# Paired attention products, shared tiles, and a last target block in two narrow passes: a change to a four-layer graph network

## The chip, the cores and the metric

The kernel runs on one core of one Trainium2 chip. The core's engines are called PE (TensorE, matmuls; PEld is its weight load), DVE (VectorE), ACT (ScalarE), POOL (GpSimd) and SP (which issues loads). SBUF is the on-chip memory, PSUM the accumulator memory that TensorE writes.

## The reference

Four layers work on 4096 nodes with 128 features and one 4096 x 4096 weighted adjacency matrix, stored in full in float32. After each layer comes a residual addition and a layer norm. The change touches the third layer (attention with 4 heads of 32 features), the end of the second, and how the fourth is run beside the third:

```
# layer 2 (the third): attention
C    = alpha_src[None, :, :] + alpha_dst[:, None, :]
tau  = adj.T[..., None] * exp(maximum(0.2 * C, C))
att  = tau / sum(tau, axis=1)
z    = einsum('mnh,nhf->mhf', adj.T[..., None] * att, h_prime) + bias
# layer 3 (the fourth)
out  = h @ W_self + (adj @ h / clip(sum(adj, 1), 1)) @ W_neigh
```

## The kernel before

A *step* takes 128 source nodes (`nt`, 32 of them), 2 heads and 1024 target nodes. ACT copies the tile `a` of the adjacency to PSUM. DVE makes two scores `tau`, maximum and multiplication in one instruction each, and part of `tau2 = tau * a`; POOL makes the rest. TensorE then adds up `den` from `tau` and `num` from `tau2`, with matmuls of 32 output columns. Thirty-two steps are a *pass*; eight passes cover 4 groups of 1024 targets and 2 pairs of heads.

```
def load(self, nt):
    if nt % 2 == 0:
        self.a2 = ld.tile([P, 2, WB], F32, name="chunk")
        nc.sync.dma_start(self.a2, adj[self.mp, nt // 2])
    a = self.a2[:, nt % 2, :]
    ap = ps_a[nt % len(ps_a)].tile([P, WB], F32, name="a")
    nc.scalar.activation(ap, a, AF.Copy, accum_out=deg[:, nt, self.mp:self.mp + 1])
    return a, ap

def products():
    if len(behind) > 1:
        heads, nt, tau, _ = behind[-2]          # den: one step behind
        heads.product(True, nt, tau)
    if len(behind) > 2:
        heads, nt, _, tau2 = behind.popleft()   # num: two steps behind
        heads.product(False, nt, tau2)
        # ... cut: end of a pass

# cut: step() = scores, the next load, then products()
while todo:
    step()
    credit = min(credit + 1.3, 2.0) if pieces else 0.0
    while credit >= 1.0:                        # matmuls of layer 3
        credit -= 1.0
        if one(pieces):
            credit = 0.0
    one(chains)                                 # small work: D, transposes, norms
```

The order on each engine is the order of this program. While the second layer's product with `w` runs on TensorE (8 blocks of 32 full matmuls), the first 46 steps are placed between its matmuls; from pass 2 on, the product of the fourth layer fills TensorE in *pieces* of one full matmul each. `tau` and `tau2` have three buffers each.

The softmax here doesn't subtract the row's maximum and nothing guards it: scores larger than these inputs give would overflow.

Of the kernel before, what the change touches and what calls it, by code (L numbers as in the profile page):

```python
# [33 lines left out]
def adj_resnorm_d4(ctx: ExitStack, tc: tile.TileContext, x_in, xT_in, adj, adjT, w0g, w0gT, a0, w1a, b1a,  # L34
# [56 lines left out]
    deg = const.tile([P, NT, NW], F32, name="deg")  # L91
# [383 lines left out]
    def network(usual):  # L475

        with ExitStack() as whole:
# [98 lines left out]

            ps_nd = enter(name="ps_nd", bufs=1, space=PSUM)
# [10 lines left out]
            def block_end(ib, p):  # L588
# [3 lines left out]
                oT = l1w.tile([P, IB], F32, name="t2T")  # L592
                nc.vector.tensor_add(oT, p, h0T[:, blk])
                elu(oT, oT, B1B)
# [34 lines left out]
            def block_targets(ib):  # L629

                blk = slice(ib * IB, (ib + 1) * IB)
                pd = ps_x.tile([96, IB], F32, name="px")
                nc.tensor.matmul(pd, WD, xT[:, blk], start=True, stop=True)
                d = l1w.tile([96, IB], F32, name="elu_r")
                nc.scalar.activation(d, pd, AF.Exp, scale=-0.8)
                nc.scalar.copy(dv[:, blk], d)
                yield
                yield
                nc.vector.tensor_sub(d, d, dv[:, blk])
                nc.scalar.copy(dv[32:64, blk], d[32:64, :])  # L640
                nc.scalar.copy(dv[64:96, blk], d[64:96, :])
                yield
                nc.vector.tensor_sub(d[64:96, :], d[64:96, :], dv[64:96, blk])
                nc.scalar.copy(dv[64:96, blk], d[64:96, :])
                yield
# [4 lines left out]
            class Heads:  # L650
# [3 lines left out]
                def __init__(self, mp, hp):  # L654
                    self.mp, self.hp = mp, hp
                    self.D, self.made = None, 0
                    self.sums = ps_first if (mp, hp) == (0, 0) else ps_nd

                def load(self, nt):

                    if nt % 2 == 0:
                        self.a2 = ld.tile([P, 2, WB], F32, name="chunk")
                        nc.sync.dma_start(self.a2, adj[self.mp, nt // 2])
                    a = self.a2[:, nt % 2, :]
                    ap = ps_a[nt % len(ps_a)].tile([P, WB], F32, name="a")
                    nc.scalar.activation(ap, a, AF.Copy, accum_out=deg[:, nt, self.mp:self.mp + 1])  # L666
                    return a, ap

                def targets(self, mbs=range(2)):
                    if self.D is None:  # L670
                        self.D = l2w.tile([P, 2, 2, IB], F32, name="D", bufs=2)
                    for mb in mbs:
                        for h in range(2):
                            d = ps_x.tile([P, IB], F32, name="px")
                            nc.tensor.matmul(d, selD[:, 2 * self.hp + h, :],
                                             dv[:, self.mp * WB + mb * IB:self.mp * WB + (mb + 1) * IB],
                                             start=True, stop=True)
                            nc.scalar.copy(self.D[:, h, mb, :], d)
                            self.made += 1
                            yield  # L680

                def step(self, nt, a, ap):

                    assert self.made == 4
                    tau = l2w.tile([P, 2, WB], F32, name="tau", bufs=3)
                    tau2 = l2w.tile([P, 2, WB], F32, name="tau2", bufs=3)
                    for h in range(2):
                        nc.vector.scalar_tensor_tensor(tau[:, h, :], self.D[:, h].rearrange("p b i -> p (b i)"),  # L688
                                                       es[:, nt, 2 * self.hp + h:2 * self.hp + h + 1], ap,
                                                       op0=ALU.max, op1=ALU.mult)  # L690
                    nc.vector.tensor_tensor(tau2[:, 0, 0:OWN], tau[:, 0, 0:OWN], ap[:, 0:OWN], ALU.mult)  # L691
                    nc.gpsimd.tensor_tensor(tau2[:, 0, OWN:WB], tau[:, 0, OWN:WB], a[:, OWN:WB], ALU.mult)  # L692
                    nc.gpsimd.tensor_tensor(tau2[:, 1, :], tau[:, 1, :], a, ALU.mult)  # L693
                    return tau, tau2

                def product(self, is_den, nt, r):
# [5 lines left out]
                    for h in range(2):  # L702
                        for mb in range(2):
                            q = 32 * (2 * h + mb)
                            nc.tensor.matmul(acc[q:q + 32, :], weights(nt, 2 * self.hp + h, is_den),  # L705
                                             r[:, h, mb * IB:(mb + 1) * IB], start=nt == 0, stop=nt == NT - 1)
                    if nt == NT - 1:
                        if is_den:
                            self.nd = l2w.tile([P, 2, IB], F32, name="nd")
                        nc.scalar.copy(self.nd[:, int(is_den), :], acc)  # L710

                def finish(self):
# [8 lines left out]
                    z = l2w.tile([P, TB, 2, 2, FO], F32, name="z")  # L721
                    nc.vector.tensor_mul(z.rearrange("p k h b f -> p (k h b) f"),
                                         q.rearrange("p k (g f) -> p (k g) f", f=FO),
                                         rd.rearrange("p k g -> p (k g)")[:, :, None].to_broadcast([P, TB * 4, FO]))
                    for mb in range(2):
                        xb = x[:, (2 * self.mp + mb) * TB:(2 * self.mp + mb + 1) * TB,
# [216 lines left out]
```

## Time and profile before

The median of before is 2280.9 us (2279.25 to 2281.45, beside the changed kernel). The end of the trace, cut by marks: t0 is DVE's addition at the end of the first block of the product with `w`; the other marks are the starts of DVE's own product (`tau2`) in steps 64, 192 and 256.

| stretch | us | what sets it |
|---|---|---|
| t0 to step 64 | 414.0 | TensorE beside the product with `w`, then DVE and ACT by turns |
| step 64 to 192 (passes 2 to 5) | 420.1 | DVE, without idle time |
| step 192 to 256 (passes 6, 7) | 213.1 | DVE, without idle time |
| step 256 to the end (tail) | 94.3 | TensorE finishing layer 3 |

### The profile page before, as it was taken

What the parts mean: (1) busy time and instruction counts of PE and PEld (TensorE: products, weight loads), DVE (VectorE), ACT (ScalarE), POOL (GpSimd) and SP (SyncE); (2) the same over time, 40 slices, a digit from 0 to 9 for tenths busy, and PEclk for the clock granted to TensorE, in tenths of its full rate; (3) what the DMA queues carried; (4) which work ended last, traced back from release to release, by engine and by line L of the source; (5) the groups of instructions that cost most, each with busy time, mean ns of one, the idle gap of its engine ahead of it and who ended that gap; (6) DMA issues with size and microseconds to landing.
All of it is one profiled execution on the core that took longest, in us unless ns stands there. A gap on an engine that the chain in (4) does not pass through costs nothing.

```text
span 2278.0 us, 22715 instructions
## 1 busy us (share of the span) xinstructions
PE 2176.3 (96%) x8552; PEld 843.0 (37%) x8552; DVE 1176.9 (52%) x1709; ACT 593.6 (26%) x1012; POOL 836.9 (37%) x540
## 2 busy tenths in 40 slices
PE   4899999999999999999999999879999999999998
PEld 3333444444444444444443333212222322232233
DVE  4554462000010110000026777779999999999955
ACT  4764200000000000000032222334444443443320
POOL 0000000000000000000004555669999999999930
PEclk9899999999999999999999999999999999999999
DMA  7886658889777677778876556434666666666665
GB/s 279 336 334 232 213 178 273 300 299 302 266 256 242 233 263 242 263 266 271 274 245 230 201 186 220 167 111 149 223 254 241 224 244 243 243 234 238 238 226 203
DMA packets 83608, 549.14 MB, mean 241 GB/s; under 512 B 9376, under 2 KB 15520, under 8 KB 17568
## 3 DMA queue, kind: packets, MB, share of 16 engines
q1 hardware_dynamic: 75200, 542.15, 68.1%
q10 hardware_dynamic: 8288, 5.44, 0.8%
q8 instruction: 69, 1.13, 0.2%
q14 instruction: 51, 0.42, 0.1%
HBM read 545.46 MB, written 2.10 MB: 240 GB/s over the span
## 4 chain that ended last, share of the span: by engine, by line
PE 83%; DVE 10%; issue 3%; ACT 2%; DMA 1%; ACTq 0%; POOL 0%; DVEq 0%; POOLq 0%
PE pacc L514 29%; PE pacc L346 10%; PE den L705 9%; PE pp L769 9%; PE pp L861 8%; PE num L705 7%; DVE tau L688 5%; DVE tau L691 2%; PE pmm L540 2%; PE num L769 1%; PE pden L334 1%; PE num L861 1%; PE px L135 1%; PE ptr L135 1%; ACT a L666 1%
## 5 line engine op out<-in xcount | busy, mean ns | idle before, releaser
L688 DVE SCALAR_TENSOR_TENSOR tau<-D,es,a 128x1024 f32<-128x1024 f32 x512 | 630.7, 1273 | 27.7 <-ACT a L666 27.5
L693 POOL TENSOR_TENSOR tau<-tau,chunk 128x1024 f32<-128x1024 f32 x256 | 609.4, 2380 | 16.7 <-DVE tau L688 15.9
L612 POOL TENSOR_TENSOR x<-x,B2R 128x512 f32<-128x512 f32 x8 | 10.2, 1279 | 1176.3 <-PE px L135 1176.3
L705 PE MATMUL den<-tau,cs 128*32 128x512 f32 x2048 | 357.0, 608 | 30.7 <-DVE tau L688 22.9
L666 ACT ACTIVATE a<-chunk 128x1024 f32<-128x1024 f32 x232 | 238.7, 1029 | 453.3 <-DVE tau L691 387.6
L705 PE MATMUL num<-tau,hc 128*32 128x512 f32 x2048 | 346.5, 600 | 0.6 <-POOL tau L693 0.6
L692 POOL TENSOR_TENSOR tau<-tau,chunk 128x320 f32<-128x320 f32 x256 | 222.8, 870 | 155.6 <-DVE tau L688 106.2
L769 PE MATMUL pp<-chunk,xT 128*128 128x512 f32 x448 | 236.1, 629 | 0.0
L691 DVE TENSOR_TENSOR tau<-tau,a 128x704 f32<-128x704 f32 x256 | 225.4, 881 | 0.0
L514 PE MATMUL pacc<-chunk,t 128*128 128x512 f32 x512 | 223.5, 592 | 0.0
L514 PE MATMUL pacc<-chunk,v 128*128 128x512 f32 x512 | 222.5, 592 | 0.0
L514 PE MATMUL pacc<-chunk,x 128*128 128x512 f32 x512 | 221.9, 592 | 0.0
L861 PE MATMUL pp<-chunk,w 128*128 128x512 f32 x448 | 208.1, 602 | 2.4 <-ACT xT L565 1.6
L346 PE MATMUL pacc<-chunk,hw 128*128 128x512 f32 x408 | 196.7, 622 | 2.3 <-DVE hw L411 2.3
L705 PEld LDWEIGHTS den<-tau,cs 128*32 128x32 f32 x2048 | 57.9, 107 | 270.2 <-DVE tau L688 180.1
L705 PEld LDWEIGHTS num<-tau,hc 128*32 128x32 f32 x2048 | 88.7, 110 | 145.0 <-issue 132.3
L514 PEld LDWEIGHTS pacc<-chunk,v 128*128 128x128 f32 x512 | 97.2, 190 | 122.0 <-issue 122.0
L514 PEld LDWEIGHTS pacc<-chunk,x 128*128 128x128 f32 x512 | 96.4, 190 | 116.7 <-issue 116.7
L514 PEld LDWEIGHTS pacc<-chunk,t 128*128 128x128 f32 x512 | 96.1, 190 | 115.3 <-issue 115.3
L769 PEld LDWEIGHTS pp<-chunk,xT 128*128 128x128 f32 x448 | 71.7, 188 | 158.6 <-issue 144.3
L561 DVE COPY w<-ptr 128x512 f32<-128x512 f32 x8 | 5.5, 691 | 241.5 <-PE ptr L135 241.5
L861 PEld LDWEIGHTS pp<-chunk,w 128*128 128x128 f32 x448 | 80.5, 190 | 115.7 <-issue 111.6
(190 smaller groups left out, 1443.5 us busy)
## 6 DMA issues: line engine op xcount, KB each, us to landing
chunk<-in_adjT SPq DMA_DIRECT2D x386, 1024.0 KB, 4.9
chunk<-in_adj SPq DMA_DIRECT2D x116, 1024.0 KB, 4.9
keep<-in_adjT SPq DMA_DIRECT2D x13, 1024.0 KB, 6.9
xT<-in_xT ACTq DMA_DIRECT2D x8, 256.0 KB, 6.1
out<-o ACTq DMA_DIRECT2D x8, 256.0 KB, 5.1
W1A<-in_w1a ACTq DMA_DIRECT2D x1, 384.0 KB, 5.6
W1B<-in_w1b ACTq DMA_DIRECT2D x1, 384.0 KB, 6.4
W0T<-in_w0gT ACTq DMA_DIRECT2D x1, 64.0 KB, 5.6
```

The lines of the kernel that those rows point to most:

```text
L135: nc.tensor.transpose(p[:, k, :], src(k), ident)
L346: nc.tensor.matmul(p, hw[:, j * TB + k, :], a[:, k, :], start=first and k == 0, stop=last and k == TB - 1)
L514: nc.tensor.matmul(p, stationary(c * TB + k), a[:, k, :], start=n == 0 and k == 0, stop=n == NB - 1 and k == TB - 1)
L540: nc.tensor.matmul(ph, W1A[:, k, hh * P:(hh + 1) * P], r, start=k == 0, stop=k == 2)
L666: nc.scalar.activation(ap, a, AF.Copy, accum_out=deg[:, nt, self.mp:self.mp + 1])
L688: nc.vector.scalar_tensor_tensor(tau[:, h, :], self.D[:, h].rearrange("p b i -> p (b i)"), es[:, nt, 2 * self.hp + h:2 * self.hp + h + 1], ap,
L691: nc.vector.tensor_tensor(tau2[:, 0, 0:OWN], tau[:, 0, 0:OWN], ap[:, 0:OWN], ALU.mult)
L692: nc.gpsimd.tensor_tensor(tau2[:, 0, OWN:WB], tau[:, 0, OWN:WB], a[:, OWN:WB], ALU.mult)
L693: nc.gpsimd.tensor_tensor(tau2[:, 1, :], tau[:, 1, :], a, ALU.mult)
L705: nc.tensor.matmul(acc[q:q + 32, :], weights(nt, 2 * self.hp + h, is_den), r[:, h, mb * IB:(mb + 1) * IB], start=nt == 0, stop=nt == NT - 1)
L769: nc.tensor.matmul(p, y[:, (2 * mp + c) * TB + k, :], a[:, k, :], start=c == 0 and k == 0, stop=c == 1 and k == TB - 1)
L861: nc.tensor.matmul(p, w[:, c * TB + k, :], a[:, k, :], start=c == 0 and k == 0, stop=c == NB - 1 and k == TB - 1)
```

## The change

Its intent is to change TensorE's tiling mode half as often, by doing the products of two steps in one visit to the narrow tiles; to use one load and copy of `a` for both first passes to their end; and to shorten the tail by taking the last 1024 targets as two passes of 512 targets and 4 heads, so that only half as much of layer 3 is left at the end. At a block's end the last ELU addition moves a slot later, and two subtractions get one input from PSUM.

```
-                todo = deque((heads, nt) for nt in range(held) for heads in passes[0:2])
-                todo += [(heads, nt) for heads in passes[0:2] for nt in range(held, NT)]
+                passes = [Pass([2 * mp, 2 * mp + 1], [2 * hp, 2 * hp + 1]) for mp in range(NW - 1) for hp in range(H // 2)]
+                passes += [Pass([b], list(range(H))) for b in range(NB - 2, NB)]
+                todo = deque((p, nt) for nt in range(NT) for p in passes[0:2])
 ... load, narrow passes:
+                        if nt % 2 == 0:
+                            self.ap2 = ps_a[nt // 2 % 2].tile([P, WB], F32, name="a").rearrange("p (t i) -> p t i", t=2)
+                        ap = self.ap2[:, nt % 2, :]
 ... products, once after two steps A and B:
+                    if len(behind) > 2:
+                        this, nt, _, tau2 = behind.popleft()
+                        num(this, nt, tau2)              # num of the B before
+                    for this, nt, tau, _ in behind:
+                        this.product(True, nt, tau)      # den of A and of B
+                    this, nt, _, tau2 = behind.popleft()
+                    num(this, nt, tau2)                  # num of A
 ... loop: chain, step A, [addition to acc], chain, step B, products, then a burst:
+                    credit = min(credit + (4.0 if todo and todo[0][0] is passes[-1] else 2.67), 4.0) if pieces else 0.0
 ... block_targets:
-                nc.vector.tensor_sub(d, d, dv[:, blk])
+                nc.vector.tensor_sub(pd, pd, dv[:, blk])   # pd is in PSUM
```

## The prediction

> **What bounds the kernel now.** I first cut the trace into stretches and read the busy time of each engine. Everything before 1206 us (layers 0 and 1 and the first three blocks of the product with `w`) is hardly touched by the change; the four stretches after it are.
>
> ```profile
> 1206.00:1470.00 264.00, 251.01 (x1128) 87.86 (x1130) 190.01 (x240) 74.79 (x140) 152.87 (x97) 0.99 0.58 206
> 1470.00:1600.00 130.00, 105.16 (x584) 25.94 (x580) 114.69 (x136) 57.65 (x114) 105.92 (x70) 0.97 0.36 122
> 1600.00:2184.00 584.00, 579.54 (x3314) 168.43 (x3310) 583.45 (x594) 233.16 (x430) 572.71 (x367) 1.00 0.67 240
> 2184.00:2278.00 94.00, 81.64 (x238) 37.04 (x230) 42.82 (x172) 9.67 (x30) 2.18 (x1) 0.97 0.59 202
> ```
>
> Columns: stretch, its length, busy us of PE, weight load, DVE, ACT, POOL, then granted clock, DMA share, GB/s. I call them C (attention steps beside the product with `w`), D (steps alone), E (steps beside the product of layer 3), F (the tail). In E, 584 us long, DVE is idle 0.6 us. PE also looks full, but its matmuls are stretched over waits. The timeline inside E shows the beat:
>
> ```profile
> 1650.71 2.47 DVE L688 SCALAR_TENSOR_TENSOR tau<-D,es,a 128x1024 f32<-128x1024 f32 x2
> 1653.09 0.88 DVE L691 TENSOR_TENSOR tau<-tau,a 128x704 f32<-128x704 f32 x1
> 1653.89 2.47 DVE L688 SCALAR_TENSOR_TENSOR tau<-D,es,a 128x1024 f32<-128x1024 f32 x2
> ```
>
> One step is 3.18 us: two scores at a pitch of 1.19 us and one product at 0.80. POOL's two products (0.87 and 2.38 us) give nearly the same. So E is bound by DVE and POOL, and TensorE savings buy nothing there.
>
> D is different: one `a` buffer in PSUM, so the copy on ACT and the DVE work alternate.
>
> ```profile
> 1488.67 2.47 DVE L688 SCALAR_TENSOR_TENSOR tau<-D,es,a 128x1024 f32<-128x1024 f32 x2 [1.29 <-ACT a L666]
> 1491.06 0.88 DVE L691 TENSOR_TENSOR tau<-tau,a 128x704 f32<-128x704 f32 x1
> 1491.98 1.03 ACT L666 ACTIVATE a<-chunk 128x1024 f32<-128x1024 f32 x1 [3.40 <-DVE tau L691]
> 1493.23 2.47 DVE L688 SCALAR_TENSOR_TENSOR tau<-D,es,a 128x1024 f32<-128x1024 f32 x2 [1.29 <-ACT a L666]
> ```
>
> There a step costs 4.56 us (1493.23 - 1488.67), 1.38 above the beat. In F, TensorE sets the pace, one output block each 7.46 us (2237.40 - 2229.94), while DVE waits 2 us of it:
>
> ```profile
> 2229.94 0.69 DVE L775 TENSOR_TENSOR acc<-pp,acc 128x512 f32<-128x512 f32 x1 [2.00 <-PE pp L769]
> 2231.19 6.17 PE L769 MATMUL num<-chunk,xT 128*128 128x512 f32 x14
> 2237.40 0.69 DVE L775 TENSOR_TENSOR acc<-num,acc 128x512 f32<-128x512 f32 x1 [1.99 <-PE num L769]
> ```
>
> **What the skill says.** "TensorEngine Tiling (Array Packing)", Key Properties, states that changing the tiling mode drains TensorE. The trace agrees: in E two instructions of the full array take 1.06 us up to the next `den` where two at the running pitch of 0.43 take 0.86, and `num` takes 0.97 up to them where `den` takes 0.88, so about 0.29 us per visit to the narrow tiles. "VectorE: DVE Perf Modes", the section on the TRN2 errata, states a fixed cost per instruction, so cutting an instruction in two pays it twice. The trace agrees: the 128-wide operation of the same kind in the output stage has a pitch of 0.28 us and the 1024-wide one 1.19, so a line through both gives 0.28 + 384 x 1.016 ns = 0.67 for 512, an estimate, more than half of 1.19. "SBUF — State Buffer", section "SBUF: two separate sides", calls the port pair of VectorE and GpSimd an exclusive lock, which a VectorE operation with two SBUF inputs needs. The trace agrees: the subtraction in `block_targets` takes 0.69 us at its shortest and 2.26 in the median of eight. The change moves one input of it to PSUM.
>
> **The change part by part.** (Orders are those of the compiled instruction lists.)
>
> *Pairing in C.* A block of 32 full matmuls takes some 52 us with nine steps now. Afterwards, blocks 3 and 4 carry four pairs, blocks 5 to 7 five. Per block: 32 x 0.86 = 27.5, transposes and small products 2.8, a pair 4 x 0.88 + 0.3 = 3.8. To this I add about 1.8 us at the block's end, where the second step's `tau` is queued on DVE behind the block's own additions (2.1 now), and 1.6 for the transposes of x, now only four matmuls behind the statistics they need. That is 49 and 52.7 us, against 52 now. Block 2 ends with a pair instead of one step (+4) and the later ELU wait saves about 2. So C ends some 1 to 2 us earlier, with 48 steps done instead of 46.
>
> *Same tiles for passes 0 and 1.* Sixteen steps are left in D, as 8 pairs on one load: 8 x (2 x 3.18 + 1.38) = 62 us, plus about 7 for the last block's statistics and exponentials in the DVE order: 69. Now step 64 ends at 1551.3; after, near 1532: **-19 us**.
>
> *Passes 2 to 7.* 192 steps keep their beat. Of them 64 become narrow: four 512-wide scores, 4 x 0.67 = 2.68 instead of 2.38, so 64 x 0.30 = **+19 us**. POOL's element counts are unchanged. The list shows 21 additions to `acc` before the last step instead of 14, and one more block of statistics: 7 x 0.6 + 2 = **+6 us**.
>
> *New waits of DVE.* The products of a pair now wait for the second step's own `tau`, then the pieces of layer 3 follow, and the addition to `acc` stands in DVE's order between the next pair's two steps. In pass 7, with four pieces a pair, the loop is: addition 0.65, scores 2.68, `den` 0.88, `num` 0.97, four matmuls and a switch 3.64 = 8.8 us, against 7.6 of DVE work. The list has 11 such pairs: 11 x 1.3 = 14. The other 10 additions wait about 0.6 each, and reciprocals behind transposes some 6 in all: 26 to 28 us. I took these from a hand-read order, and the kernel before hides nearly all such waits in E, so I count half: **+14 us**.
>
> *Tail.* TensorE has 44 full matmuls in F instead of 79 (158 records of two each), and one block to finish instead of two. The bound passes to DVE, whose work for an output block is about 4.4 us (addition 0.75, scale and statistics 2.25, normalization 1.35), and whose list now interleaves blocks. First addition of the last product about 18 us after the last `num`, eight blocks x 4.5, and 5.3 from the last DVE operation to the end: 59 us against 91 now (2187.2 to 2278): **-31 us** after rounding for the later `num`.
>
> Sum: -19 + 19 + 6 + 14 - 31 = -11, so 2270 us.
>
> **Rivals.** (1) TensorE was the hidden bound of E: its busy share is 99%, and the chain that ended last runs more through PE than DVE. Then 96 pairs save up to 0.3 us and idle disappears: about 2240. Against it: DVE idle 0.6 us of 584, and its durations are not stretched. (2) The pair's waits count in full, as the hand-read loop says: +14 more, about 2284, or 2300 if waits meet the reciprocals. For it: strict program order on DVE; against it: three buffers of `tau` let DVE run ahead. (3) Loads in halves of 2 KB rows hold back the narrow passes. Pass 7 needs about 1.5 MB per 7.5 us, 200 GB/s, below the 240 that E carries now, so I expect nothing; if they did, +10. (4) The tail stays bound by TensorE or loads: 44 x 0.86 plus transposes is 43 us, so it would still gain 25.
>
> **Range and chances.** The two gains (-19, -31) are read directly; the losses of 39 can lie between 20 and 65, and C can differ by 8. That gives 2240 to 2298. Two per cent faster means 2235, which needs nearly no loss in the narrow passes: 0.09. Slower than 2326 needs a wait I did not see: 0.03.
>
> **What would show it.** Right: the beat in wide passes stays near 6.4 us per pair with DVE full; narrow scores have a pitch near 0.67; in pass 7 DVE idles before `acc`, released by PE; pass 2 begins near 1532; output blocks come every 4.5 us. Wrong: the beat falls below 6.3 us, or DVE idle in E is over 40 or under 5 us, or C ends over 8 us away from now.

## More of the kernel before

The time is the device time of one execution in microseconds (us).

In the list of TensorE's waits in passes 2 to 5 of the kernel before (columns: what waited, for what, us in total, times, longest) there are three lines; DVE's own list for this stretch is empty.

```profile
PE den L705 <- DVE tau L688: 2.1, 4, 0.7
PE px L750 <- ACT x L756: 0.4, 2, 0.2
PE den L705 <- ACT nd L710: 0.2, 1, 0.2
```

So both engines run without gaps, 420 us long.

## The result, and the profile after

The changed kernel takes 2339.6 us in the median (2336.18 to 2344.93, 4 runs); its ratio to the kernel before is 1.0261, 95% interval 1.0241 to 1.0281: it is slower by 2.6%. 2270 was predicted, with a range up to 2298. By the marks:

| stretch | before | predicted | after |
|---|---|---|---|
| t0 to step 64 | 414.0 | 395.5 | 417.2 |
| step 64 to 256 | 633.2 | 672 | 724.8 |
| tail | 94.3 | 63 | 62.0 |

(Predicted: 1532 - 1136.5, where t0 is 1136.5 in the trace of before; 633.2 + 19 + 6 + 14; 94.3 - 31.) The tail came out as foreseen. The other two missed by 22 and 53 us.

Stretches of the changed kernel, in the columns of the prediction's first view (stretch, length, then busy us of PE, PEld, DVE, ACT and POOL, granted clock, DMA share, GB/s):

```profile
1195.00:1482.00 287.00, 270.96 (x1173) 94.78 (x1175) 194.26 (x245) 78.10 (x145) 157.19 (x100) 1.00 0.56 195
1482.00:1552.00 70.00, 50.19 (x262) 10.93 (x258) 58.73 (x67) 19.50 (x36) 52.73 (x34) 0.90 0.18 61
1552.00:2008.00 456.00, 426.64 (x2432) 122.86 (x2436) 423.41 (x439) 176.60 (x334) 414.73 (x267) 0.99 0.62 220
2008.00:2276.00 268.00, 254.72 (x1249) 80.77 (x1242) 235.46 (x364) 55.43 (x164) 207.82 (x131) 1.00 0.43 146
2276.00:2338.00 62.00, 49.23 (x160) 23.16 (x158) 40.08 (x164) 6.66 (x20) 2.36 (x1) 0.91 0.48 160
```

The third and fourth lines are the former E. DVE was idle 0.6 us there; now it is idle 456.00 - 423.41 = 32.6 us in passes 2 to 5 and 268.00 - 235.46 = 32.5 us in passes 6 and 7. So most of the time was lost to waits. The work grew too, as foreseen: DVE's busy time in the last two passes rose by about 23 us, from 212.8 to 235.5, and the prediction had 25 for that.

Three places show the waits. First, TensorE beside the product with `w` (timeline: start, us, engine, line, operation; in brackets the idle time before and its releaser). One visit to the narrow tiles for two steps:

```profile
1319.46 1.07 PE L731 MATMUL num<-tau,hc 128*32 128x512 f32 x8
1320.35 1.04 PE L731 MATMUL den<-tau,cs 128*32 128x512 f32 x8
1321.89 1.81 PE L731 MATMUL den<-tau,cs 128*32 128x512 f32 x6 [0.50 <-DVE tau L709]
...
1324.10 0.14 PEld L731 LDWEIGHTS num<-tau,hc 128*32 128x32 f32 x4 [0.86 <-POOL tau L715]
...
1325.09 3.70 PE L888 MATMUL pp<-chunk,w 128*128 128x512 f32 x8
```

The visit takes 5.63 us (1325.09 - 1319.46). Its second `den` is that of step B, whose `tau` DVE is only just making, so TensorE stands still within the visit. A second operand is late as well: the last loads for the `num` of step A wait 0.86 us for the product that POOL makes.

Second, the loop in the passes beside layer 3. These are the lines of one round, by engine:

```profile
1774.26 0.88 DVE L713 TENSOR_TENSOR tau<-tau,a 128x704 f32<-128x704 f32 x1
...
1776.24 2.84 PE L794 MATMUL pp<-chunk,xT 128*128 128x512 f32 x6
...
1778.92 0.38 PE L695 MATMUL px<-dv,selD 96*128 96x512 bf16 x1
...
1779.33 0.58 ACT L696 COPY D<-px 128x512 f32<-128x512 f32 x1 [3.25 <-PE px L695]
1779.82 1.03 ACT L686 ACTIVATE a<-chunk 128x1024 f32<-128x1024 f32 x1
...
1781.05 2.47 DVE L709 SCALAR_TENSOR_TENSOR tau<-D,es,a 128x1024 f32<-128x1024 f32 x2 [2.73 <-issue]
```

Read it downwards: the visit ends, late because it waited for B; then comes the burst of layer 3 (1776.24), behind it a small product (1778.92), whose copy to `D` ACT has to make (1779.33) before its next copy of `a` (1779.82), for which DVE waits 2.73 us. (The profile names no releaser for that wait, "issue"; the reading rests on the copy's end, 1779.82 + 1.03 = 1780.85, just before DVE starts at 1781.05.) The Trainium skill, "PSUM — Partial Sum Buffer", section "Engine vs sequencer instructions", says that the queues of ScalarE, VectorE and GpSimd are strictly first in, first out, and that TensorE's matmuls start and complete in program order. The trace agrees: the copy of `a` needed nothing from the small product and still came 0.49 us after the start of the copy that did.

DVE's waits in passes 2 to 5, where the kernel before has none:

```profile
DVE tau L709 <- issue: 13.5, 7, 2.7
DVE acc L799 <- PE pp L794: 6.4, 8, 0.8
DVE tau L709 <- POOL tau L715: 6.3, 3, 2.5
DVE tau L709 <- ACT a L686: 2.9, 2, 1.6
```

Third, the narrow passes, DVE and ACT together:

```profile
2023.06 0.88 DVE L719 TENSOR_TENSOR tau<-tau,a 128x704 f32<-128x704 f32 x1
...
2026.49 0.88 DVE L719 TENSOR_TENSOR tau<-tau,a 128x704 f32<-128x704 f32 x1
...
2028.22 2.72 DVE L709 SCALAR_TENSOR_TENSOR tau<-D,es,a 128x512 f32<-128x512 f32 x4 [0.69 <-ACT a L686]
2030.87 0.88 DVE L719 TENSOR_TENSOR tau<-tau,a 128x704 f32<-128x704 f32 x1
```

```profile
2027.40 0.60 ACT L686 ACTIVATE a<-chunk 128x512 f32<-128x512 f32 x1 [5.98 <-DVE tau L719]
```

Steps follow one another after 3.43 us (2026.49 - 2023.06) and 4.38 us (2030.87 - 2026.49) by turns. (The wait is 0.94 us; DVE fills 0.25 of it with a small reciprocal, so the view shows 0.69.) Both steps of a pair have their `a` in one PSUM tile, and the copy of the second half (2027.40) starts only when the first step's last reader has finished (2026.49 + 0.88 = 2027.37).

And the tail, DVE's additions for successive output blocks:

```profile
2302.53 0.66 DVE L799 TENSOR_TENSOR acc<-num,acc 128x512 f32<-128x512 f32 x1
...
2306.92 0.65 DVE L799 TENSOR_TENSOR acc<-pp,acc 128x512 f32<-128x512 f32 x1
...
2311.30 0.65 DVE L799 TENSOR_TENSOR acc<-num,acc 128x512 f32<-128x512 f32 x1
```

One block takes 4.4 us instead of 7.46, and these three additions no longer wait for TensorE.

### The profile page after: what moved, and what is told of

Read it like the earlier page. It is cut to its first block, busy times and chain, and to the rows that moved or that the text cites. A ratio compares the mean times of both kernels' runs of the same rounds, so it can differ in the third digit from the quotient of the medians.

```text
span 2338.1 us, 22778 instructions
## 1 busy us (share of the span) xinstructions
PE 2202.1 (94%) x8552; PEld 851.9 (36%) x8552; DVE 1198.6 (51%) x1844; ACT 551.5 (24%) x996; POOL 838.9 (36%) x539
## 5 line engine op out<-in xcount | busy, mean ns | idle before, releaser
L709 DVE SCALAR_TENSOR_TENSOR tau<-D,es,a 128x1024 f32<-128x1024 f32 (+1 forms) x640 | 646.6, 1059 | 59.7 <-issue 25.2
L731 PE MATMUL den<-tau,cs 128*32 128x512 f32 x2048 | 389.4, 602 | 54.3 <-DVE tau L709 45.4
L731 PE MATMUL num<-tau,hc 128*32 128x512 f32 x2048 | 365.8, 608 | 1.4 <-POOL tau L715 1.4
L686 ACT ACTIVATE a<-chunk 128x1024 f32<-128x1024 f32 (+1 forms) x224 | 202.9, 906 | 496.9 <-DVE tau L713 287.0
L794 PE MATMUL pp<-chunk,xT 128*128 128x512 f32 x480 | 227.3, 608 | 0.3 <-DVE acc L799 0.3
L714 POOL TENSOR_TENSOR tau<-tau,chunk 128x320 f32<-128x320 f32 x192 | 167.1, 870 | 141.4 <-DVE tau L709 99.2
L731 PEld LDWEIGHTS den<-tau,cs 128*32 128x32 f32 x2048 | 83.2, 109 | 332.2 <-DVE tau L709 242.2
L713 DVE TENSOR_TENSOR tau<-tau,a 128x704 f32<-128x704 f32 x192 | 168.6, 878 | 0.0
L514 PEld LDWEIGHTS pacc<-chunk,x 128*128 128x128 f32 x512 | 96.4, 190 | 116.7 <-issue 116.7
L794 PEld LDWEIGHTS pp<-chunk,xT 128*128 128x128 f32 x480 | 84.6, 189 | 139.1 <-issue 135.9
L731 PEld LDWEIGHTS num<-tau,hc 128*32 128x32 f32 x2048 | 71.5, 109 | 164.7 <-issue 99.1
```

Source lines behind the costliest of these rows:

```text
L514: nc.tensor.matmul(p, stationary(c * TB + k), a[:, k, :], start=n == 0 and k == 0, stop=n == NB - 1 and k == TB - 1)
L686: nc.scalar.activation(ap, a, AF.Copy, accum_out=deg[:, nt, s:s + 1])
L709: nc.vector.scalar_tensor_tensor(flat(tau[:, q:q + n]), flat(self.D[:, q:q + n]), es[:, nt, head:head + 1], ap, op0=ALU.max, op1=ALU.mult)
L713: nc.vector.tensor_tensor(t2[:, 0:OWN], t[:, 0:OWN], ap[:, 0:OWN], ALU.mult)
L714: nc.gpsimd.tensor_tensor(t2[:, OWN:WB], t[:, OWN:WB], a[:, OWN:WB], ALU.mult)
L731: nc.tensor.matmul(acc[32 * q:32 * q + 32, :], weights(nt, head, is_den), r[:, q, :], start=nt == 0, stop=nt == NT - 1)
```

## The experiments

There were three theories of the miss: (1) two narrow steps share a PSUM tile; (2) `den` waits for its own `tau`; (3) the burst of layer 3 holds up small products and, behind them, ACT's copies. The rival to all three was that TensorE is simply full, or that the narrow passes alone are the loss. Unless said otherwise each kernel gave a correct result and was timed in 3 rounds, 4 runs; the kernel before had medians of 2279.1 to 2282.0 beside them. Stage times are from the traces.

| run | t0 to step 64 | 64 to 192 | 192 to 256 | tail | median us | ratio to before |
|---|---|---|---|---|---|---|
| before | 414.0 | 420.1 | 213.1 | 94.3 | 2280.9 | 1 |
| after | 417.2 | 456.2 | 268.6 | 62.0 | 2339.6 | 1.0261 |
| own_tile | 417.5 | 456.3 | 256.9 | 62.1 | 2333.4 | 1.0236 |
| den_behind | 396.5 | 435.1 | 253.1 | 60.7 | 2280.9 | 1.0012 |
| all_wide | 417.4 | 456.2 | 225.1 | 82.4 | 2318.3 | 1.0175 |
| split_burst | 417.4 | 440.1 | 262.4 | 62.2 | 2321.9 | 1.0185 |
| behind_own | 396.5 | 435.2 | 236.0 | 60.5 | 2268.2 | 0.9955 |
| behind_own_split | 396.5 | 428.5 | 235.9 | 62.4 | 2263.2 | 0.9928 |
| singles | 380.5 | 425.2 | 232.4 | 81.2 | 2258.5 | 0.9906 |
| singles_apart | 385.7 | 420.0 | 232.5 | 82.8 | 2259.6 | 0.9919 |
| singles_wide | 380.5 | 425.2 | 213.1 | 85.6 | 2243.4 | 0.9837 |
| singles_fast | 380.5 | 428.2 | 241.2 | 60.0 | 2244.4 | 0.9837 |
| deep_pairs | 381.6 | 434.7 | 239.0 | 58.1 | 2251.8 | 0.9870 |
| deep_pairs_320 | 381.6 | 434.7 | 236.1 | 57.8 | 2248.8 | 0.9847 |
| before_own_tau | 479.9 | 437.8 | 221.0 | 95.4 | 2373.1 | 1.0412 |
| singles_scattered | 382.6 | 425.0 | 232.5 | 81.5 | 2260.9 | 0.9914 |
| best_320 (5 rounds) | 380.5 | 428.2 | 239.5 | 57.5 | 2247.5 | 0.9845 |
| singles_sbuf_sub | 387.8 | 424.9 | 232.5 | 81.2 | 2264.0 | 0.9938 |
| singles_old_elu | 385.8 | 425.0 | 232.5 | 81.3 | 2264.1 | 0.9928 |

The medians also hold the stretch before t0, which varied by 13 us for reasons that no run shows, so medians a few us apart should be checked against the sum of the four stages. These sums are 1141.5 us for before, 1204.0 for after, 1192.8 for own_tile, 1145.4 for den_behind, 1113.4 for deep_pairs, 1109.9 for singles_fast, 1105.7 for best_320 and 1104.4 for singles_wide (one trace each).

### own_tile

```
-                        if nt % 2 == 0:
-                            self.ap2 = ps_a[nt // 2 % 2].tile([P, WB], F32, name="a").rearrange(...)
-                        ap = self.ap2[:, nt % 2, :]
+                        ap = ps_a[nt % 2].tile([P, WB], F32, name="a")[:, 0:IB]
```

> The changed kernel, but in the narrow passes each step copies its 512 columns of a to a PSUM tile of its own, instead of two steps sharing one. Theory 1: the copy for the second step of a pair waits until the first step's readers of the shared tile are done, 0.94 us in each of 32 pairs. Then pass 6 (16 pairs) gets about 15 us shorter (pair pitch 6.87 instead of 7.80) and pass 7 about 5 (its five pairs without an addition; the eleven others are held by the loop through TensorE, 8.8 us): 2339 - 20 = 2319, range 2308 to 2324. Rival: the copy was late for ACT's own order (its copies stand behind D copies and products), then the time stays within 3 us of 2339.

2333.4 us: between the two (6 us by the medians, 11 by the stages). The mechanism is as theory 1 has it. In pass 6 the marks of DVE's own product now follow one another evenly, at 3.43 us:

```profile
2022.47 0.89 DVE L717 TENSOR_TENSOR tau<-tau,a 128x704 f32<-128x704 f32 x1
...
2025.90 0.89 DVE L717 TENSOR_TENSOR tau<-tau,a 128x704 f32<-128x704 f32 x1
...
2029.33 0.89 DVE L717 TENSOR_TENSOR tau<-tau,a 128x704 f32<-128x704 f32 x1
```

But the size was not: pass 6 got 9.9 us shorter (127.6 to 117.7), not 15, and pass 7 only 1.8 (141.0 to 139.2), not 5. In the two passes the waits of the addition to `acc` for TensorE stayed, 15.6 us before and 16.6 after: where that loop holds the pair back, an earlier copy brings nothing.

### den_behind

```
-                    if len(behind) > 2: num of the B before
-                    den of A and of B
-                    num of A
+                    while len(behind) > 1:
+                        this, nt, tau, tau2 = behind.popleft()
+                        this.product(True, nt, tau)     # the B before, then A
+                        num(this, nt, tau2)
```

> The changed kernel, but a visit of TensorE to the narrow tiles takes den of the step before and of the first step of the pair, so never of the step whose tau DVE is just making; num stays one step behind as well. Theory 2: den waiting for its own tau costs 14 us in the stretch beside the product with w (step 48 ends at 1481, then near 1467) and most of the 36 us by which passes 2 to 5 got longer (457 us, then 430 or less), also some of pass 7: 2339 - 45 = 2294, range 2275 to 2310. Rival: TensorE's own work per pair fills the beat and the waits of DVE come from ACT, which holds the next copies behind small products; then step 48 comes earlier all the same, but passes 2 to 5 keep at least 20 of their 36 us: above 2310.

2280.9 us, 59 us less than the changed kernel and 14 more than the expected 45, though within its range. The stretch up to step 64 gave 21 us, passes 2 to 5 gave 21 and pass 7 gave 15. Of the 36 us that passes 2 to 5 had gained in length 15 stayed, short of the rival's 20. TensorE no longer waits for `tau` in passes 2 to 5; what is left is `num`, waiting for POOL:

```profile
PE num L731 <- POOL tau L715: 15.6, 22, 1.2
```

### all_wide

```
-                passes = [... for mp in range(NW - 1) ...]
-                passes += [Pass([b], list(range(H))) for b in range(NB - 2, NB)]
+                passes = [... for mp in range(NW) ...]
```

The rate of pieces is 2.67 a pair throughout, without the 4 of the last pass.

> The changed kernel with pairs and shared tiles, but all eight passes of 2 heads and 1024 nodes. If the narrow passes cost what the trace shows (30 us shared tile, 19 us narrower scores, 6 us more additions, some 10 of the loop in pass 7) and return 32 us in the tail: passes 6 and 7 together near 232 us instead of 268, the tail 94 instead of 62, and 2337 in all, range 2325 to 2350. A rival that puts the loss on the narrow passes alone says that this variant comes back to 2281.

2318.3 us, a miss of the expectation's range by 7: the last 64 steps took 225 us instead of 232, and the tail 82 instead of 94, since the pairs' rate of pieces leaves less of layer 3 than the kernel before had left (132 records of its matmuls behind the last `num` in the trace, against 162; two records are one full matmul). Narrow passes alone are not the loss: 37 us of it stay without them.

### split_burst

```
+                    burst()          # half the matmuls of layer 3
                     one(chains)
                     step()           # step B
                     products()
+                    burst()          # the other half
```

> The changed kernel, but the three (in the last pass four) matmuls of layer 3 in a row are cut: half after the first step of a pair, half after the second. Theory 3: in ACT's strict order a copy that waits for a small product behind the burst holds back the next copies of a, which makes most of the 33 us of DVE idle in passes 2 to 5. With half the burst ahead of it, passes 2 to 5 get 12 to 20 us shorter, and 2339 becomes about 2322 (2312 to 2330). If instead den's wait for its own tau is the cause, TensorE has no more work to fill that wait with than now, and the change is under 6 us.

2321.9 us, as theory 3 expects: passes 2 to 5 got 16 us shorter, with TensorE still waiting for B's `tau` (14.6 us before, 13.8 now). So the burst is a second link by which a late visit reaches DVE. How much of the 16 went through ACT's copies is not shown: in DVE's list for these passes the wait of the addition to `acc` went from 6.4 us to nothing, while the waits put down to "issue" only fell from 13.5 to 11.1. Up to step 64, where there is no burst, nothing moved (417.2 and 417.4).

### behind_own and behind_own_split

These kernels join the edits shown: den_behind with own_tile, then split_burst as well.

> den one step behind (as in den_behind) and a PSUM tile of its own for each narrow step's a (as in own_tile). Theory: the shared tile alone cost only 11 us, because in pass 7 (and partly in pass 6) the loop through den and the addition to acc was there to take over. With that loop gone, all 32 pairs get 0.8 to 0.94 us shorter: passes 6 and 7 together from 253 to about 228 us, 2281 becomes 2256, range 2248 to 2264. Rival: something else (POOL, its port lock, PE's visits) holds the narrow pair at 7.8 us too; then passes 6 and 7 stay above 240 and the time above 2268.

2268.2 us, 4 above its range. Passes 6 and 7 went from 253 to 236 us, so the PSUM tile that was worth 12 in own_tile is worth 17 here; that lies between the theory's 228 and the rival's 240. In passes 2 to 7 DVE is idle 15.4 us in this kernel (671 less 655.6 busy).

> The three mended together: den one step behind, own PSUM tile, burst of layer 3 cut in two. Theory: the 15 us that passes 2 to 5 still have over the kernel before (435 against 420 us) are the small products behind the burst, whose copies hold back ACT; cutting the burst takes 8 to 14 us of them. About 2245, range 2236 to 2256, that is 1.1 to 2.0 per cent below the kernel before. If den behind and the cut burst mend the same wait, it is the same as behind_own within 4 us.

2263.2 us. The cut burst takes 6.7 us off passes 2 to 5, not 8 to 14; in passes 6 and 7 it gives nothing, and the whole kernel misses its range by 7. Together, waits mended by den_behind and by the cut burst overlap: 16 us alone, 7 after the other.

### singles

```
     def products():
-        (the pair's version)
+        if len(behind) > 1: den of behind[-2]
+        if len(behind) > 2: num of the oldest
 ... called after every step; 1.33 pieces of layer 3 and one chain a step; own_tile's load
```

> The changed kernel's passes (same tiles for the first two, narrow last two with an own PSUM tile), but the products of each step by themselves, den one step behind, num two, 1.33 pieces of layer 3 a step, as in the kernel before. It shows what pairing is worth. TensorE then has 2 visits a pair instead of one, 0.29 us more, and its work per pair is near DVE's 6.36: if pairing gains, this is 5 to 15 us slower than behind_own_split; if pairing is worth nothing because DVE sets the beat, they are the same within 4 us, near 2245.

2258.5 us, better than behind_own_split by 5, which neither side had expected: no pairs at all, and faster than every pair so far. The stages say where: 16 us up to step 64 and 3 to 4 in each of the next two stretches, against 19 lost in the tail. Passes 3 to 5 take 102.5, 106.9 and 104.9 us, which is the kernel before to 0.1 us (102.5, 107.0 and 104.9). Pairing gains nothing where DVE sets the beat. The tail is 81 us because fewer of the pieces ran early enough: the trace has 121 records of layer 3's matmuls behind the last `num`, the changed kernel 85, and singles_fast below, with 67, brings the tail back to 60.

One more thing came with the singles: `num` runs two steps behind again, where the pair (and den_behind) takes `num` of A one step behind. In den_behind TensorE waited for POOL's product 15.6 us in passes 2 to 5 and 5.1 up to step 48; in singles neither list has such a wait, and the stretches are 10 and 16 us shorter than in den_behind. deep_pairs below, which keeps pairs and the full burst but takes `num` two steps behind, points the same way (318.4 us in passes 3 to 5 against 324.1 in den_behind). No run changes the lag of `num` alone, so its share is likely but not shown.

Beside the product with `w` the singles still place two steps together, so that TensorE sees this:

```profile
1309.29 1.06 PE L729 MATMUL den<-tau,cs 128*32 128x512 f32 x8
1310.17 1.04 PE L729 MATMUL num<-tau,hc 128*32 128x512 f32 x8
1311.03 1.04 PE L729 MATMUL den<-tau,cs 128*32 128x512 f32 x8
1311.89 1.04 PE L729 MATMUL num<-tau,hc 128*32 128x512 f32 x8
1312.86 3.70 PE L885 MATMUL pp<-chunk,w 128*128 128x512 f32 x8
```

It is the same work as in the visit of the changed kernel shown above, two `den` and two `num`, in 3.57 us (1312.86 - 1309.29) instead of 5.63. The difference is which steps they belong to: here all four operands were finished, there `tau` of B and POOL's part of A were not.

### singles_apart

```
-                todo = deque((p, nt) for nt in range(NT) for p in passes[0:2])
+                todo = deque((p, nt) for nt in range(held) for p in passes[0:2])
+                todo += [(p, nt) for p in passes[0:2] for nt in range(held, NT)]
```

> As singles, but the last 16 steps of the first two passes in the order of the kernel before: eight steps of one pass, then eight of the other, each with its own load and copy. It shows what the same tiles are worth. Each of these steps then waits 1.3 to 1.4 us for the copy where with the same tiles one in two does: 8 x 1.38 = 11 us slower than singles, range 8 to 14. Rival: chains of the last block fill the same waits, then under 5.

2259.6 us against 2258.5, where 8 to 14 more was expected: the same tiles are worth next to nothing in the end. Up to step 64 they gain 5.2 us (380.5 against 385.7); pass 2 takes 5.1 more (110.9 against 105.8). The traces suggest why, though no run separates it: with passes 0 and 1 interleaved both end together, so the second PSUM buffer for `a` comes later and the chains of both fall into pass 2.

### singles_wide and singles_fast

singles_wide is singles with all_wide's list of passes (the wide steps have had a PSUM tile each all along). singles_fast changes the rate:

```
-                    credit = min(credit + (2.0 if ... is passes[-1] else 1.335), 3.0) ...
-                    (credit thrown away at the end of a sum)
+                    credit = min(credit + (2.0 if ... in passes[-2:] else 1.335), 3.0) ...
+                    (kept; the addition to acc comes behind the next step's scores)
```

> As singles (products of each step by themselves, den one step behind), but all eight passes wide: it takes the narrow passes out of a kernel that has no waits of the pairs. Theory: the narrow passes cost DVE work only, 232 us instead of 213 for the last 64 steps, and save TensorE work in the tail. Here passes 6 and 7 take 213 us as in the kernel before and the tail about 92 to 95: 2258 - 19 + 12 = 2251, range 2243 to 2258; the rest of what singles gains over the kernel before (30 us by step 64) then belongs to the stretch beside the product with w. If narrow passes were the whole gain of singles, it is near 2281.

2243.4 us, the low end. Passes 6 and 7 take 213.1 us, exactly as in the kernel before, and the narrow ones 232.4: they cost 19 us of DVE. The tail is 85.6.

> As singles, but in the last two passes 2 pieces of layer 3 a step, and the credit isn't thrown away at the end of a sum: 32 full matmuls are left after the last num instead of 59. Theory: the tail of singles (81 us against 61 in the paired kernels) is this rest alone, so it falls to 57 to 62 and the time to 2237, range 2230 to 2246. TensorE's work per narrow step (2.1 + 2 x 0.86 = 3.8 us) then is near DVE's 3.5 to 3.6: if it takes the bound, passes 6 and 7 get up to 8 us longer than 232.

2244.4 us. The tail falls to 60.0, and passes 6 and 7 grow to 241.2: the pieces must be done somewhere, and in pass 7 (124.5 us instead of 116.3) TensorE takes the bound: its records fill 124.4 of the 124.5 us, while DVE is idle 4.4. So, at these rates of pieces, splitting the last 1024 targets nets nothing against wide passes, +28 in the passes (241.2 - 213.1) and -26 in the tail (60.0 - 85.6).

### deep_pairs and deep_pairs_320

```
                     step()
                     products()       # den one, num two steps behind
                     step()
                     products()       # in one visit: nothing for PE in between
                     one(chains)
                     burst of 2.67 (4 in the last two passes)
                     one(chains)
 320:
-                        own = OWN // 2
+                        own = OWN // 2 - 32
```

> Products of two steps in one visit of TensorE, but den one and num two steps behind for both, so that the visit waits for nothing new; pieces and rates as in singles_fast. Theory: taking two steps together was not itself the fault, what was taken was: this runs as singles_fast or up to 4 us faster, 2235, range 2228 to 2244. Rival: any pairing hurts, because three or four full matmuls in a row hold up the small products and with them ACT's copies: then it is 8 us or more slower than singles_fast.

2251.8 us: 7 us slower than singles_fast by the medians, between the theory and its rival, but only 4 by the stages. No `den` of B is asked of TensorE too soon here, yet passes 2 to 5 take 434.7 us against 428.2. The trace says where: pass 2 alone takes 116.4 us against 110.9, and its first steps wait 4.8 us for copies to `D`, which this edit's order of small products brings later:

```profile
1525.58 1.28 DVE L707 SCALAR_TENSOR_TENSOR tau<-D,es,a 128x1024 f32<-128x1024 f32 x1 [3.64 <-ACT D L694]
```

Passes 3 to 5 take 318.4 us against 317.2. So in these passes pairing with the right operands gains nothing and costs 1.2 us; the loss is at the start of pass 2. In pass 7, where singles_fast has TensorE at its bound, the pairs take 120.4 us against 124.5, but pass 6 went the other way (118.6 against 116.7), so a gain there is not shown.

> deep_pairs with 320 instead of 352 columns of each of the two products done by DVE in the narrow passes (POOL takes the other 192). DVE then needs 3.41 us a narrow step instead of 3.48, POOL 3.40 instead of 3.25. Up to 4 us faster than deep_pairs; the same within 2 if TensorE or POOL sets the narrow beat; slower by 3 or more if POOL's products take longer than their element count says.

2248.8 us. Passes 6 and 7 are 2.9 us shorter than in deep_pairs, the medians differ by 3.1 with overlapping ranges (2240.2 to 2250.7 and 2249.3 to 2254.7).

### before_own_tau

The kernel before with theory 2's fault alone, and no pair anywhere:

```
-                    if len(behind) > 1:
-                        heads, nt, tau, _ = behind[-2]
-                        heads.product(True, nt, tau)
+                    heads, nt, tau, _ = behind[-1]
+                    heads.product(True, nt, tau)
```

> The kernel before with one edit: den of a step is taken right after this step's own scores instead of one step later; nothing is paired, nothing else is changed. Theory: den's wait for a tau that DVE is just making is what costs, in pairs or not, because TensorE has almost no slack in a step (2.1 us of products with their switch, 1.3 x 0.86 of layer 3, small products) and must idle until the scores are done: passes 2 to 5 get 20 us or more longer than 420, and step 48 comes 10 us or more later; 2281 becomes 2310 to 2370. Rival: only the pair makes it dear (two den and a burst behind the wait): then under 2295.

2373.1 us, 4.1% slower than the kernel before, above even the changed kernel and just above the expected range. This is the clearest run: `den` asked for one step too early costs 93 us by itself. Step 46 comes 395.3 us after t0 instead of 332.1; passes 2 to 5 are 17.7 us longer, a little short of the 20 expected. TensorE's waits between 1215 and 1540 us, and one of them:

```profile
PE den L705 <- DVE tau L688: 44.8, 17, 4.0
```

```profile
1303.48 2.26 PE L705 MATMUL den<-tau,cs 128*32 128x512 f32 x6 [2.04 <-DVE tau L688]
```

Beside the product with `w` the fault is worse without pairs (63 us over 46 steps) than with them (18 us over 48: 347.4 to step 48 in the changed kernel, 329.0 in den_behind), where one of two `den` is early. One early `den` of two would explain a half, but not less than a third; the rest of the difference was not looked into.

### singles_scattered, singles_sbuf_sub, singles_old_elu

Up to step 64 singles is 33 us ahead of the kernel before, far more than the prediction gave to this stretch. Three runs each undo one thing: the placing of two steps together, the subtraction from PSUM, and the later ELU addition.

```
 scattered:
-                        if steps and todo[0][1] < min(ready, held): step, products, (chain), step, products
+                        for n in range(int(ib > 2 or (ib, c) == (2, NB - 1)) + int(ib > 2 and end)): step, products
 sbuf_sub:
-                nc.scalar.activation(pd, pd, AF.Exp, scale=-0.8)
-                nc.vector.tensor_sub(pd, pd, dv[:, blk])
+                nc.scalar.activation(d, pd, AF.Exp, scale=-0.8)
+                nc.vector.tensor_sub(d, d, dv[:, blk])
 old_elu:
-                ... exp; yield; nc.vector.scalar_tensor_tensor(oT, n, -1.0, r, ...); yield
+                elu(oT, oT, B1B); yield
```

> singles with the steps beside the product with w placed as in the kernel before, one after most groups of four full matmuls, so that TensorE visits the narrow tiles for one step at a time; the new chains at a block's end stay. If two steps in one place (one visit, products that wait for nothing) is what makes this stretch 29 us shorter than before: 15 to 29 us come back, 2273 to 2287, and step 46 comes near 332 us after the first block's end (before: 332). If the new chains (later ELU addition, subtraction from PSUM, order at a block's end) are the reason: step 46 comes near 303 as in singles, and 2258 stays within 6.

2260.9 us. Step 46 comes at 307.3 after t0, 4 us later than in singles (303.2) and 25 earlier than before. So two steps in one place are worth 2 to 6 us there (2.1 at step 64, 6.0 at step 48). The prediction gave more: its 1 to 2 us came with two more steps done, which is some 11 us at step 48 (341.8 before, about 330 predicted).

> singles with the two subtractions of block_targets on SBUF tiles again, as in the kernel before. If VectorE with two SBUF inputs and GpSimd exclude one another, the subtractions take 2.2 to 2.3 us again instead of 0.70 wherever POOL is at work: some 8 to 10 of them, 1.5 us each, 12 to 15 us of DVE. Where TensorE's den runs one step behind, part of it is hidden: step 48 comes 3 to 12 us later than 313 after the first block's end. If it is hidden altogether: under 2 us.

2264.0 us. Step 48 comes 5.0 us later, step 64 7.3 later. (The edit moves the output of ACT's exponential to SBUF as well; its share was not separated.) The Trainium skill, "SBUF — State Buffer", section "SBUF: two separate sides", says that a VectorE operation with two SBUF inputs and a GpSimd operation that reads SBUF exclude one another for a whole instruction. The timelines agree: the subtraction of the third block on SBUF takes 2.26 us (first line, this run) and on PSUM 0.70 (second line, singles). POOL is in the middle of a product beside both, from 1229.75 to 1232.10 us in the one trace and from 1232.51 to 1234.87 in the other; the subtraction on SBUF ends 0.54 us after POOL's product, the one on PSUM ends within it.

```profile
1230.38 2.26 DVE L646 TENSOR_TENSOR elu_r<-elu_r,dv 96x512 f32<-96x512 f32 x1
```

```profile
1233.26 0.70 DVE L645 TENSOR_TENSOR px<-px,dv 96x512 f32<-96x512 f32 x1
```

> singles with the ELU of a block in one go again, as in the kernel before: its last addition stands on DVE right behind the sum, waits there for ACT's exponential (0.8 us), but then finds POOL idle more often (0.69 us instead of 2.28). If the later slot is what pays: step 48 comes 5 to 25 us later than 313. If it is only moved: within 3 us, and the 29 us lie in the order of chains and steps at a block's end.

2264.1 us; step 48 comes 5.7 us later, step 64 5.3 later. So the later slot pays (at the low end of the 5 to 25 expected), although the addition itself now mostly takes 2.26 us instead of 0.69 beside POOL. The three together come to 2.1 + 7.3 + 5.3 = 14.7 of the 33 us by step 64; the rest, in the order of chains at a block's end and the same tiles (5.2), was not taken apart further.

### best_320

It has singles' products, rates as in singles_fast, credit thrown away before the last two passes, and the 320 columns.

> The parts that paid, together: products of singles, pieces of layer 3 in passes 2 to 5 at the old rate with the credit thrown away at a sum's end, 2 a step in the last two passes, 320 columns of the own product for DVE. From singles_fast (2244): passes 2 to 5 get 3 us back, passes 6 and 7 some 2 to 4: 2239, range 2232 to 2245, that is 1.8 per cent below the kernel before.

2247.5 us (2237.5 to 2249.5, 5 runs), 2.5 above its range: by the medians no better than singles_wide or singles_fast, by the stages some 4 us better than singles_fast, in the last two passes and the tail; the 3 us of passes 2 to 5 did not come back (428.2), so the thrown-away credit was not what separates them. The best versions are singles_wide and singles_fast, 1.6% below the kernel before (ratio 0.9837 each, 0.9812 to 0.9863 and 0.9811 to 0.9863), a gain clear of noise.

## Why the prediction was wrong

**Sum.** It missed by 69 us (2339.6 - 2270). Two edits take back what it did not see: den_behind 59 us, and then the own PSUM tile another 13 (2280.9 to 2268.2). The kernel with both, behind_own, takes 2268.2 where 2270 was predicted, and its stretches are 396.5, 671.2 and 60.5 us where 395.5, 672 and 63 were. That agreement is partly luck. In 671.2 two errors cancel: passes 2 to 5 take 435.2 us where the prediction left them near 420, and passes 6 and 7 take 236.0 where it had 238 of work and up to 14 of waits. In 396.5, two gains that it gave little or nothing (the subtractions from PSUM and the later ELU slot, 5.0 and 5.7 us at step 48 in the singles) stand against waits that singles, at 380.5, no longer has. What it priced well is the work in the narrow passes, the tail and the sixteen steps of D.

It gave 0.03 to a time over 2326, which "needs a wait I did not see". That came true.

**The step that failed** is the price of one wait: the products of a pair "now wait for the second step's own `tau`". The prediction counted it at the ends of blocks in C (1.8 us each), halved it in pass 7 and all but left it out in passes 2 to 5. den_behind, which changes only which `den` the visit takes, measured it: 21 us up to step 64, 21 in passes 2 to 5, 15 in pass 7. A reading of the profile lies behind this: it said that TensorE only looks full, its matmuls "stretched over waits". TensorE's list has 2.7 us of waits in passes 2 to 5. And from the prediction's own figures, as an estimate, a step beside layer 3 asks 3.17 us of TensorE (`den` 0.88, `num` with the switch after it 0.97, 1.3 full matmuls of 0.86, the switch back 0.20), of the 3.18 that the step lasts. Nothing was left to absorb a wait.

**Pairing in C.** It added "about 1.8 us at the block's end, where the second step's `tau` is queued on DVE" and 1.6 for the transposes, as if the wait occurred once per block. It occurs within the blocks too: up to step 48 the trace lists 16 waits of TensorE for `tau`, 11.2 us, and step 48 came at 347.4 us after t0, where about 330 had been worked out (1467 - 1136.5). With `den` one step behind it came at 329.0. The prediction said that the products of a pair "now wait for the second step's own `tau`", and took no cost per pair from it here.

**Same tiles.** The sixteen steps in D were to take 69 us and took 69.8 (48 to 64), so the working of this stretch was right. The sum with C was not: C's end near 1467 and 69 us give 1536, not 1532, so -15 and not -19 by its own terms. What was wrong besides is what it was worth: the -19 includes C's end, and the tiles themselves gained 5.2 us which pass 2 gave back.

**Narrow passes.** The score's pitch is (2026.49 - 2023.86)/4 = 0.66 us, predicted 0.67. The +19 for the scores and +6 for additions and statistics stand against 23 us more DVE busy time. Unseen, and in no term of the sum, was the shared PSUM tile: 12 us by itself (268.6 to 256.9), 17 once `den` was out of the way. The rearranged tile was in the diff, and I read only the instructions' order, where the wait doesn't show.

**New waits.** For pass 7 the hand-read loop, 11 additions at 1.3 us, was close: over the last two passes the trace has 13 such waits, 15.6 us together, the longest 1.4. "So I count half" was wrong: the reason given, that the kernel before hides nearly all such waits, holds for `den` one step behind, which is just what the change gave up. And passes 2 to 5 had no term beyond some 0.6 us an addition. They lost 36 us: den_behind gives back 21 of it and split_burst after that 7, so they came by the loop from `den` over the burst to DVE. Of the last 8 some 5 are probably the slower pass 2 that the same tiles bring (110.9 us against 105.8 in the singles).

**Tail.** -31 predicted, -32.3 measured, with blocks every 4.4 us.

**Rivals.** (1) TensorE as the hidden bound, which fewer visits would relieve, falls: deep_pairs makes half as many visits as singles_fast and passes 3 to 5 take 318.4 us against 317.2, and den_behind is 59 us faster with the same work on TensorE. It is full enough, though, that its waits are passed on. (2) Waits in full, at 2284 to 2300, was the right kind and too small. (3) Loads of 2 KB rows: with an own tile the pitch in pass 6 is 3.43 us, DVE's own work, so they hold back nothing there. (4) The tail did not stay bound by TensorE. Of the prediction's own signs of error two came true: DVE was idle 65 us in E, over 40, and C's last step came 13 us away (1481.4 + 0.8 against 1468.6 + 0.8), over 8.

## What to carry to other kernels

When two steps' work is moved together, ask of each operand when it was made: give an engine that has no slack only what was finished a step ago. before_own_tau shows that one step's lag was worth 93 us here. A term like "waits, halved" hides loops; write down a round of the loop over all engines in their strict order, and see that every buffer in it belongs to one step. A cost that is mended alone may show only part of its worth (12 us, then 17), so test the parts together too.

## What the Trainium skill lacked or had wrong

- "TensorEngine Tiling (Array Packing)", Key Properties, names the drain at a change of tiling mode without a figure. Here a visit costs about 0.29 us for it, while a visit that waits for an unfinished operand lost 2.06 us (5.63 - 3.57).
- "PSUM — Partial Sum Buffer", section "Engine vs sequencer instructions", has the strict order of the queues right. It doesn't say what follows: a copy on ACT that waits for one small matmul delayed an unrelated one, and DVE behind it by 2.73 us. split_burst, with less work in front of such matmuls, got 16 us back in four passes, not all of it shown to be by this link.
- No page was found that warns of two steps sharing one PSUM tile in two halves: the copy into the second half waited until the readers of the first had finished (2027.40 after 2027.37), 12 to 17 us in all. A tile for each step removed the wait (own_tile); the runs don't show what the memory would allow within one tile.
